# Two attention layers on eight images: output projections in another order, the norm among products, and the first attention begun on half of q and k

## The chip, the cores and the metric

The kernel runs on one core of one Trainium2 chip. Its time is the time on the device in microseconds (us), the median of several runs; the kernel before took 4062.5 us in the median of three runs (4062.24 to 4063.74). The profile is one execution, with a span of 4059.8 us from first to last instruction. TensorE (PE) multiplies matrices, VectorE (DVE), ScalarE (ACT) and GpSimd (POOL) do the rest, and SyncE (SP) issues nearly all transfers. [...]

## The reference, cut to what matters

Eight images of 32 x 32 positions with 512 channels, all fp32, go through two layers. Each normalises in 32 groups of channels, runs an attention over the 1024 positions and adds the result to its input.

```python
# layer 0: 16 heads of 32
xt = gn(x).reshape(B, N, C)
q, k, v = split_heads(xt @ w_qkv)
attn = softmax((q * 32 ** -0.5) @ k.T)
x = x + (attn @ v) @ w_proj + b_proj
# layer 1: 4 heads of 128, relative positions along both axes
q, k, v = gn(x) @ Wq / sqrt(128), gn(x) @ Wk, gn(x) @ Wv
scores = q @ k.T + relative_logits(q, pos_emb_w, pos_emb_h)
x = x + (softmax(scores) @ v) @ Wo
```

Each image has eight 512 x 512 projections: q, k, v and output in both layers.

## The kernel before

**Projections.** All activations lie with channels on the partitions, four chunks of 128 channels by 1024 positions. A projection is done in two half units, each by `seven` (L328): seven block products where a plain scheme has eight, on sums and differences of quarters ("forms", four VectorE operations in `forms`, L311 to L324, into three fixed buffers and in place). Unit u gives chunks u and u + 2 of the result. A product is eight matmuls, which the trace shows as 16 records (each fp32 matmul is recorded twice), in line L299. Around the products stand ScalarE copies of a half-done sum out of PSUM (p1, p7), VectorE adds (a, b) and the four adds or copies that give the result's quarters, by a "sink": `Plain` writes a new block, `Onto` (from L410) adds onto the residual. Half-done sums of products share three PSUM banks with other work. The pieces of weight for each product come from `Stream`, which loads them a unit ahead through 16 buffers, in the order of one list, `plan`; the list must match the order in which the units are done.

**First attention** (`attention_0`, L506): 64 steps, four chunks of heads by two halves of queries by eight blocks of keys. A step is scores `ps` (L516, eight matmul records, one PSUM buffer), an exponential `e` on ScalarE (L524, two buffers), the weighted sum of values `acc` (L535) and, on VectorE, the running sum of exponentials `es` (L544, L546). After eight steps `sums` (L556) and `normalise` (L482 to L504) divide the chunk. The second attention, `attention_1`, works likewise on heads of 128.

**Order of the work.** The main loop has nine iterations. Iteration b runs `attention_0(b)` side by side with a chain of other work. `side_by_side` (L782) advances the chain as far as a running account of costs allows: a product counts 2, the sum of the chain's costs is `total`, and after attention step n the chain may have used n/65 of it. What is left of the chain when the attention ends is done after it. In the middle iterations, the chain of before is:

1. the second layer's output projection of image b-2 (`after_1`; weights WO), at whose sixth product of the second unit a hook (`forms_0`) makes the forms of image b-1's first attention output
2. the first layer's output projection of image b-1 (`after_0`; WP), with the statistics for the norm
3. the norm of image b-1 (`norm_1`: store the block, ten small VectorE operations, and four L282 over the chunks), each of its pieces priced at ALONE = 5, so that only attention steps lie beside it
4. q, k, v of the second layer with the position logits (`second`; WQ1, WK1, WV1), starting with forms of the normed block
5. the second attention, woven with the loading, turning and norm of image b+1 (`load`)
6. q, k and v of the first layer for image b+1 (`before_0`), with a hook for the forms of the second attention's output

In front of the loop stands `before_0(0)`, so q, k and v of image 0 are done alone; iteration 0 then has the first attention of image 0 beside the loading of image 1 and its q, k, v. The residual inputs are stored in DRAM and come back by `fetch`, four transfers of 512 KB each, into blocks of which there are eight.

A scheduler puts the final order on each engine; it keeps to program order but for waits it can foresee and for stretches under `high_priority`.

Of the kernel before, what the change touches and what calls it, by code (L numbers as in the profile page):

```python
# [17 lines left out]
P = 128  # L18
# [9 lines left out]
def quick_path(  # L28
# [131 lines left out]
    class Stream:  # L160


        def __init__(self, plan):
            self.plan = [(m, rows, u) for m, rows in plan for u in range(2)]
            self.tiles = {}
            self.at = -1
            for i in ORDER:
                self.load(0, i)
# [77 lines left out]
    def group_norm(st, xT, name):  # L246

        mv = st.pop("mv")

        def averages(out, src, tag):  # L250
            total = small.tile([P, 2], F32, tag=f"total{tag}", name=f"total{tag}_{name}")
            nc.vector.tensor_reduce(
                total, src.rearrange("p (g k) -> p g k", k=GROUP_CHANNELS), axis=AX.X, op=ALU.add
            )
            nc.vector.tensor_scalar(
                out.rearrange("p (g k) -> p g k", k=GROUP_CHANNELS),
                total.unsqueeze(2).to_broadcast([P, 2, GROUP_CHANNELS]),
                1.0 / GROUP_CHANNELS,
                None,
                op0=ALU.mult,  # L260
            )

        turned = small.tile([P, 32], F32, tag="turned", name=f"turned_{name}")
        nc.vector.transpose(turned, mv)
        avg = small.tile([P, 2, 32], F32, tag="avg", name=f"avg_{name}")
        averages(avg[:, 0, :], turned, 0)

        nc.vector.tensor_sub(turned, turned, avg[:, 0, :])
        nc.vector.tensor_mul(turned, turned, turned)
        averages(avg[:, 1, :], turned, 1)  # L270
        back = small.tile([P, 2, 32], F32, tag="back", name=f"back_{name}")
        nc.vector.transpose(back.rearrange("p a c -> p (a c)"), avg.rearrange("p a c -> p (a c)"))
        mean = back[:, 0, :CC]
        var = small.tile([P, CC], F32, tag="var", name=f"var_{name}")
        nc.vector.scalar_tensor_tensor(
            var, back[:, 0, CC : 2 * CC], GN_EPS, back[:, 1, :CC], op0=ALU.add, op1=ALU.add
        )
        rstd = small.tile([P, CC], F32, tag="rstd", name=f"rstd_{name}")
        nc.gpsimd.tensor_tensor(rstd, var, neg_half, op=ALU.pow)
        yield 0  # L280
        for cc in range(CC):
            nc.vector.tensor_scalar(  # L282
                xT[cc],
                xT[cc],
                mean[:, cc : cc + 1],
                rstd[:, cc : cc + 1],
                op0=ALU.subtract,
                op1=ALU.mult,
            )
        yield 0  # L290


    in_place = [False]
# [31 lines left out]
    def snapshot(tag, name):  # L325
        return mem.tile([P, NB], F32, tag=tag, name=name, bufs=3 if tag == "e1" else 2)

    def seven(fs, u, rows, sink, name, hook=None):  # L328

        def product(out, i, start):
            w, f = stream.take(i), fs[i]
            if not rows:
                for c in range(HC):
                    by_columns(out, w[c], f[:, c, :], start and c == 0, c == HC - 1, True)
            else:
                for t in range(2):
                    for c in range(HC):  # L340
                        by_columns(
                            out[:, t * HN : (t + 1) * HN],
                            f[:, c, (2 * u + t) * P : (2 * u + t + 1) * P],
                            w[c],
                            start and c == 0 and t == 0,
                            c == HC - 1,
                            True,
                        )
            stream.ahead(i)

        x = bank(f"x_{name}")
        product(x, 0, True)
        p1 = snapshot("e1", f"p1_{name}")
        nc.scalar.copy(p1, x)
        yield HC
        y = bank(f"y_{name}")
        product(y, 5, True)
        a = snapshot("es1", f"a_{name}")
        nc.vector.tensor_add(a, y, p1)
        sink.early(p1, a)  # L360
        yield HC
        product(x, 1, False)
        sink.c11(x)
        yield HC
        product(y, 4, False)
        b = snapshot("es1", f"b_{name}")
        nc.vector.tensor_add(b, y, p1)
        sink.middle(b)
        yield HC
        z = bank(f"z_{name}")  # L370
        product(z, 6, True)
        p7 = snapshot("e1", f"p7_{name}")
        nc.scalar.copy(p7, z)  # L373
        yield HC
        product(y, 2, False)
        sink.c12(y, p1)
        if hook is not None:
            hook()
        yield HC
        product(z, 3, False)  # L380
        sink.c21(z, a)
        sink.c22(b, p7)
        yield HC

    class Plain:
# [64 lines left out]

        return [[x[n * HC + u][:, h * NB : (h + 1) * NB] for h in range(NH)] for n in range(2)]

    def project_T(fs, m, y, name):

        for u in range(2):
            stream.unit(m, False, u)
            yield from seven(fs, u, False, Plain(halves(y, u)), f"{name}_{u}")

# [46 lines left out]

    def attention_0(q, k, v, b):  # L506

        steps = [(m, h, j) for m in range(CC) for h in range(NH) for j in range(NT)]
        state = {}

        def front(m, h, j):
# [163 lines left out]
    def load(b, st):  # L675
# [19 lines left out]
        st["xn"] = forms(x, f"xn0_{b}")  # L695
        yield 0

    def before_0(b, st, hook=None):

        fs = st.pop("xn")  # L700
        st["q0"] = block(f"q0_{b}")
        st["q"] = chunks(st["q0"])
        yield from project_T(fs, WQ0, st["q"], f"q0_{b}")
        st["k"] = chunks(block(f"k0_{b}"))
        yield from project_T(fs, WK0, st["k"], f"k0_{b}")
        st["v"] = block(f"v0_{b}", [P, NT, C])
        yield from project_rows(fs, WV0, st["v"], f"v0_{b}", hook)
# [103 lines left out]
    PRODUCT = 2 * len(ORDER) * HC  # L811
    SECOND = 3 * PRODUCT - 8

    ALONE = 5

    WQ0, WK0, WV0 = [Matrix(w_qkv, i * C, f"qkv{i}") for i in range(3)]
    WP, WQ1, WK1 = Matrix(w_proj, 0, "p"), Matrix(Wq, 0, "q1"), Matrix(Wk, 0, "k1")
    WV1, WO = Matrix(Wv, 0, "v1"), Matrix(Wo, 0, "o")
    FIRST = [(WQ0, False), (WK0, False), (WV0, True)]
    plan = list(FIRST)  # L820
    for b in range(B + 1):
        if b == B:
            plan.append((WP, False))
        if b >= 2:
            plan.append((WO, False))
        if 1 <= b < B:
            plan.append((WP, False))
        if b >= 1:
            plan += [(WQ1, False), (WK1, False), (WV1, True)]
        if b + 1 < B:  # L830
            plan += FIRST
    plan.append((WO, False))

    states = [{} for _ in range(B)]
    WQ0.add_up(nc.vector, nc.scalar, nc.gpsimd, keep=True)
    run(load(0, states[0]))
    for m in (WK0, WV0):
        m.add_up(nc.vector, nc.sync, nc.gpsimd, keep=True)
    stream = Stream(plan)

# [2 lines left out]
            m.add_up(nc.gpsimd, nc.gpsimd, nc.gpsimd)  # L843
            yield 0

    run(before_0(0, states[0]))
    for b in range(B + 1):
        rest, total = [], 0
        s = [None] * 2 + states + [None] * 2
        past, last, here, coming = s[b : b + 4]  # L850
        incoming = load(b + 1, coming) if coming is not None else iter(())

        def forms_0(b=b, st=last):
            st["ao0"] = forms(st["q0"], f"ao0_{b - 1}")

        def forms_past(b=b, st=past):
            forms_1(b - 2, st)

        def forms_last(b=b, st=last):
            forms_1(b - 1, st)  # L860

        if last is not None:
            norm = norm_1(b - 1, last)
            if here is None:
                rest.append(after_0(b - 1, last, forms_past))
                rest.append(woven(later(after_1, b - 2, past), norm, 1, 4))
            else:
                if past is not None:
                    rest.append(after_1(b - 2, past, forms_0))
                    total += PRODUCT  # L870
                rest.append(later(after_0, b - 1, last))
                rest.append(chain([ALONE], (cost + ALONE for cost in norm), marked()))
                total += PRODUCT + 3 * ALONE
            rest.append(later(second, b - 1, last))
            rest.append(woven(later(lambda st: attention_1(*st.pop("at")), last), incoming, 4, 6))
            total += SECOND
        else:
            rest.append(incoming)
        if coming is not None:
            before = later(before_0, b + 1, coming, forms_last if last is not None else None)  # L880
            rest.append(before if last is not None else woven(before, other_sums(), 2, 7))
            total += 3 * PRODUCT
        if here is not None:
            side_by_side(attention_0(here["q"], here["k"], here["v"], b), chain(*rest), total)
        else:
            run(chain(*rest))
# [493 lines left out]
```

## Time and profile before

| engine | busy us | share | instructions |
|---|---|---|---|
| TensorE | 3848.8 | 95% | 30338 |
| VectorE | 2531.9 | 62% | 2915 |
| ScalarE | 1719.5 | 42% | 1761 |
| GpSimd | 601.6 | 15% | 396 |

| what | number of instructions | busy us |
|---|---|---|
| first attention: exponentials L524 | 512 | 961.6 |
| first attention: running sums L546 and L544 | 384 + 64 | 899.3 + 173.1 |
| TensorE's waits for exponentials ahead of scores L516 | 60 waits | 127.3 |
| DMA moved | 234.18 MB | mean 58 GB/s |

The busy time of an engine is the union of its instructions' times; matmuls overlap in it, so that a busy TensorE need not be one at its peak. In brackets behind an instruction stand the idle time of its engine just before it and what ended it. The granted clock (PEclk) is the share of full speed that TensorE's throttle allowed, 0.983 in the mean of the span.

### The profile page before, as it was taken

How to read it: one execution, taken by the hardware profiler on the slowest of the kernel's cores; microseconds unless marked ns; L12 is line 12 of the kernel's file. 1: busy time of each engine (PE TensorE's matmuls, PEld its weight loads, DVE VectorE, ACT ScalarE, POOL GpSimd, SP SyncE). 2: the span in 40 equal slices, each digit the busy share in tenths (PEclk: the TensorE clock that was granted, in tenths of full speed). 3: DMA queues.
4: the chain of work that ended last, by engine and by line, in shares of the span. 5: the costliest groups of instructions: out<-in, count | busy, mean ns of one | idle time of the engine just before them, and what ended most of it. 6: DMA issues, size and time to landing. Idle time of an engine off the chain costs nothing.

```text
span 4059.8 us, 71621 instructions
## 1 busy us (share of the span) xinstructions
PE 3848.8 (95%) x30338; PEld 1417.6 (35%) x30338; DVE 2531.9 (62%) x2915; ACT 1719.5 (42%) x1761; POOL 601.6 (15%) x396
## 2 busy tenths in 40 slices
PE   6898899998999989999999999999999998999998
PEld 3232244232443324432244323433234332244353
DVE  5776665576655867458564685646856568664544
ACT  1454443444434444344443444444444444543132
POOL 1331111121111211112110111101111111111101
PEclk9999999999999999999999999999999999999999
DMA  5320120141201512014120231203311031110401
GB/s 143 118 86 26 48 59 6 37 122 50 59 6 38 129 49 58 7 47 131 37 53 12 88 85 36 53 19 95 79 37 45 26 98 54 33 63 8 115 29 22
DMA packets 498694, 234.18 MB, mean 58 GB/s; under 512 B 286368, under 2 KB 478144, under 8 KB 497344
## 3 DMA queue, kind: packets, MB, share of 16 engines
q1 hardware_dynamic: 495232, 214.79, 19.8%
q0 software_dynamic: 2608, 13.70, 0.9%
q8 instruction: 241, 3.95, 0.4%
q10 hardware_dynamic: 528, 1.05, 0.1%
q14 instruction: 85, 0.70, 0.1%
HBM read 170.72 MB, written 58.72 MB: 57 GB/s over the span
## 4 chain that ended last, share of the span: by engine, by line
PE 86%; DVE 7%; ACT 5%; issue 1%; DMA 1%; POOL 0%; SPq 0%; DVEq 0%; ACTq 0%; POOLq 0%
PE ps L516 12%; PE ps L626 11%; PE acc L638 11%; PE acc L535 11%; PE y_q L299 4%; PE y_k L299 3%; PE y_v L299 3%; PE ps L627 3%; ACT e L524 3%; PE x_v L299 3%; PE x_k L299 3%; PE x_q L299 3%; PE z_q L299 3%; PE z_v L299 2%; PE z_k L299 2%; PE y_wp L299 2%
## 5 line engine op out<-in xcount | busy, mean ns | idle before, releaser
L524 ACT ACTIVATE e<-ps 128x2048 f32<-128x2048 f32 x512 | 961.6, 1878 | 873.4 <-PE ps L516 749.1
L546 DVE TENSOR_TENSOR es<-es,e 128x2048 f32<-128x2048 f32 x384 | 899.3, 2342 | 504.5 <-ACT e L524 503.0
L516 PE MATMUL ps<-q,k 32*128 32x512 f32 x4096 | 613.1, 654 | 127.5 <-ACT e L524 127.3
L535 PE MATMUL acc<-e,v 128*32 128x512 f32 x4096 | 557.5, 617 | 12.9 <-ACT su L482 11.9
L629 ACT ACTIVATE e<-ps 128x512 f32<-128x512 f32 x512 | 305.7, 597 | 581.4 <-PE ps L627 551.2
L626 PE MATMUL ps<-q,k 128*128 128x512 f32 x1024 | 523.7, 593 | 0.0
L638 PE MATMUL acc<-e,v 128*128 128x512 f32 x1024 | 521.9, 592 | 0.0
L649 DVE TENSOR_TENSOR es<-es,e 128x512 f32<-128x512 f32 x384 | 287.0, 747 | 267.3 <-ACT e L629 266.5
L627 PE MATMUL ps<-posT,sel 128*128 128x512 f32 x512 | 406.7, 794 | 0.0
L504 POOL TENSOR_TENSOR q<-q,su 128x512 f32<-128x512 f32 x128 | 199.2, 1557 | 1381.7 <-DVE su L500 1339.3
L516 PEld LDWEIGHTS ps<-q,k 32*128 32x128 f32 x4096 | 166.6, 186 | 533.4 <-ACT e L524 267.2
L626 PEld LDWEIGHTS ps<-q,k 128*128 128x128 f32 x1024 | 193.6, 190 | 246.2 <-issue 239.4
L638 PEld LDWEIGHTS acc<-e,v 128*128 128x128 f32 x1024 | 193.1, 189 | 146.7 <-issue 105.2
L535 PEld LDWEIGHTS acc<-e,v 128*32 128x32 f32 x4096 | 82.0, 109 | 409.3 <-issue 352.1
L612 DVE TENSOR_TENSOR posT<-pp,posT 32x512 fp32r<-32x512 f32 x128 | 111.2, 869 | 157.8 <-ACT posT L611 157.3
L544 DVE TENSOR_TENSOR es<-e,e 128x2048 f32<-128x2048 f32 x64 | 173.1, 2704 | 35.7 <-ACT e L524 35.7
L484 DVE STREAM_TRANSPOSE tu<-su 128x512 f32<-128x512 f32 x128 | 90.7, 709 | 116.3 <-ACT su L482 116.0
L611 ACT CAST posT<-pp 32x512 fp32r<-32x512 f32 x128 | 104.8, 819 | 132.2 <-DVE posT L612 87.4
L482 ACT COPY su<-sums 128x512 f32<-128x512 f32 x128 | 74.9, 585 | 160.2 <-PE sums L556 92.1
L408 POOL TENSOR_TENSOR v<-b_v,p_v 128x512 f32<-128x512 f32 x32 | 67.3, 2104 | 499.8 <-ACT p_v L373 479.3
L408 POOL TENSOR_TENSOR k<-b_k,p_k 128x512 f32<-128x512 f32 x32 | 64.0, 1999 | 513.7 <-ACT p_k L373 513.7
L627 PEld LDWEIGHTS ps<-posT,sel 128*128 128x128 f32 x512 | 97.3, 190 | 122.5 <-issue 122.5
(188 smaller groups left out, 4404.1 us busy)
## 6 DMA issues: line engine op xcount, KB each, us to landing
w_qkv<-ws_qkv SPq DMA_DIRECT2D x168, 128.0 KB, 2.5
xs<-in_x SPq DMA_DIRECT2D x256, 64.0 KB, 2.6
d<-x0T SPq DMA_DIRECT2D x32, 512.0 KB, 3.0
x1T<-d SPq DMA_DIRECT2D x32, 512.0 KB, 6.4
d<-x1T SPq DMA_DIRECT2D x32, 512.0 KB, 3.6
x2T<-d SPq DMA_DIRECT2D x32, 512.0 KB, 6.0
out<-ot SPq DMA_DIRECT2D x256, 64.0 KB, 2.0
w_qkv<-in_L_conv_w_qkv SPq DMA_DIRECT2D x126, 128.0 KB, 2.2
```

Source lines behind the costliest of these rows:

```text
L299: ins = nc.tensor.matmul(out[columns, :], weights[:, columns], moving, start=start, stop=stop, skip_group_check=open_sum,)
L504: nc.gpsimd.tensor_tensor(dst, dst, su, op=ALU.mult)
L516: nc.tensor.matmul(ps[:, r, :], k[m][rows, j * P : (j + 1) * P], q[m][rows, h * NB : (h + 1) * NB], start=True, stop=True,)
L524: nc.scalar.activation(e, ps, AF.Exp, scale=D0 ** -0.5)
L535: nc.tensor.matmul(acc[r * D0 : (r + 1) * D0, :], v[:, j, c0 : c0 + D0], e[:, r, :], start=(j == 0), stop=(j == NT - 1),)
L544: nc.vector.tensor_add(state["esum"], state["first"], e)
L546: nc.vector.tensor_add(state["esum"], state["esum"], e)
L626: nc.tensor.matmul(ps, k[h][:, keys], q[:, h, queries], start=True, stop=False)
L627: nc.tensor.matmul(ps, sel[:, keys], posT[:, h, queries], start=False, stop=True)
L629: nc.scalar.activation(e, ps, AF.Exp, scale=1.0 / math.sqrt(D1))
L638: nc.tensor.matmul(acc, v[:, j, h * D1 : (h + 1) * D1], e, start=(j == 0), stop=(j == NT - 1),)
L649: nc.vector.tensor_add(state["esum"], state["esum"], e)
```

## The change

The output projections change places: the first layer's, of image b-1, comes ahead of the second layer's, of image b-2. The norm of image b-1 then no longer has to stand between a projection and q of the second layer: it is woven into the second layer's output projection, from the fourth product on, a piece every third. The norm of a block comes in more pieces (a yield after every second chunk). Hooks move with that: the forms for `after_1` are made at the end of `after_0`, and those for `after_0` at the end of `before_0`, where the total of an iteration is cut by seven products so that the first attention ends ahead of them. Iteration 1 has no second-layer projection yet and keeps the norm alone (ALONE 4, four pieces).

In front of the loop, v and half of q and k of image 0 are done first; the attention takes its chunks in the order 0, 2, 1, 3, needing only the first unit's chunks for its first half, and the second half of q and k is done beside it, woven with the loading of image 1.

In `seven`, the copies and adds that read half-done sums are put down at a raised priority (SOON = 100).

```diff
-        yield 0
+            if cc % 2:
+                yield 0
...
+    SOON = 100
...
-        nc.scalar.copy(p1, x)
+        with tc.high_priority(SOON):
+            nc.scalar.copy(p1, x)
...
-        sink.c11(x)
+        with tc.high_priority(SOON):
+            sink.c11(x)
...
-        steps = [(m, h, j) for m in range(CC) for h in range(NH) for j in range(NT)]
+        steps = [(m, h, j) for m in (0, 2, 1, 3) for h in range(NH) for j in range(NT)]
...
+    def before_first(st):
+        fs = st["xn"]
+        st["v"] = block("v0_0", [P, NT, C])
+        yield from project_rows(fs, WV0, st["v"], "v0_0")
...
+        yield from project_T(fs, WQ0, st["q"], "q0_0", (0,))
+        yield from project_T(fs, WK0, st["k"], "k0_0", (0,))
+
+    def rest_of_first(st):
+        fs = st.pop("xn")
+        yield from project_T(fs, WQ0, st["q"], "q0_0", (1,))
+        yield from project_T(fs, WK0, st["k"], "k0_0", (1,))
...
-    ALONE = 5
+    ALONE = 4
...
-    run(before_0(0, states[0]))
+    run(before_first(states[0]))
...
         if last is not None:
             norm = norm_1(b - 1, last)
-            if here is None:
-                rest.append(after_0(b - 1, last, forms_past))
-                rest.append(woven(later(after_1, b - 2, past), norm, 1, 4))
+            rest.append(after_0(b - 1, last, forms_past if past is not None else None))
+            total += PRODUCT
+            if past is not None:
+                rest.append(woven(later(after_1, b - 2, past), norm, 3, 3))
+                total += PRODUCT
             else:
-                if past is not None:
-                    rest.append(after_1(b - 2, past, forms_0))
-                    total += PRODUCT
-                rest.append(later(after_0, b - 1, last))
                 rest.append(chain([ALONE], (cost + ALONE for cost in norm), marked()))
-                total += PRODUCT + 3 * ALONE
+                total += 4 * ALONE
             rest.append(later(second, b - 1, last))
+            total += SECOND
+            if here is not None and coming is None:
+                rest.append(at_once(forms_0))
+                total -= 4
             rest.append(woven(later(lambda st: attention_1(*st.pop("at")), last), incoming, 4, 6))
-            total += SECOND
         else:
-            rest.append(incoming)
+            rest.append(woven(rest_of_first(here), incoming, 0, 2))
+            total += PRODUCT
         if coming is not None:
-            before = later(before_0, b + 1, coming, forms_last if last is not None else None)
+            before = later(before_0, b + 1, coming, forms_0 if last is not None else None)
...
-            total += 3 * PRODUCT
+            total += 3 * PRODUCT - (PRODUCT // 2 if last is not None else 0)
```

More of the change, by code (lines that the diff above doesn't have):

```diff
@@ L163, in __init__ @@
         def __init__(self, plan):
-            self.plan = [(m, rows, u) for m, rows in plan for u in range(2)]
+            self.plan = plan
             self.tiles = {}
@@ L358, in seven @@
         a = snapshot("es1", f"a_{name}")
-        nc.vector.tensor_add(a, y, p1)
+        with tc.high_priority(SOON):
+            nc.vector.tensor_add(a, y, p1)
         sink.early(p1, a)
@@ L362, in seven @@
         product(x, 1, False)
-        sink.c11(x)
+        with tc.high_priority(SOON):
+            sink.c11(x)
         yield HC
@@ L366, in seven @@
         b = snapshot("es1", f"b_{name}")
-        nc.vector.tensor_add(b, y, p1)
+        with tc.high_priority(SOON):
+            nc.vector.tensor_add(b, y, p1)
         sink.middle(b)
@@ L372, in seven @@
         p7 = snapshot("e1", f"p7_{name}")
-        nc.scalar.copy(p7, z)
+        with tc.high_priority(SOON):
+            nc.scalar.copy(p7, z)
         yield HC
         product(y, 2, False)
-        sink.c12(y, p1)
+        with tc.high_priority(SOON):
+            sink.c12(y, p1)
         if hook is not None:
@@ L380, in seven @@
         product(z, 3, False)
-        sink.c21(z, a)
-        sink.c22(b, p7)
+        with tc.high_priority(SOON):
+            sink.c21(z, a)
+            sink.c22(b, p7)
         yield HC
@@ L451, in halves, with project_T @@
         return [[x[n * HC + u][:, h * NB : (h + 1) * NB] for h in range(NH)] for n in range(2)]
-    def project_T(fs, m, y, name):
-        for u in range(2):
+    def project_T(fs, m, y, name, units=(0, 1)):
+        for u in units:
             stream.unit(m, False, u)
@@ L696, in load @@
         yield 0
+    def before_first(st):
+        fs = st["xn"]
+        st["v"] = block("v0_0", [P, NT, C])
+        yield from project_rows(fs, WV0, st["v"], "v0_0")
+        st["q0"] = block("q0_0")
+        st["q"] = chunks(st["q0"])
+        st["k"] = chunks(block("k0_0"))
+        yield from project_T(fs, WQ0, st["q"], "q0_0", (0,))
[4 more added lines that the diff above has]
+        yield from project_T(fs, WK0, st["k"], "k0_0", (1,))
     def before_0(b, st, hook=None):
@@ L818, in quick_path, with units @@
     WV1, WO = Matrix(Wv, 0, "v1"), Matrix(Wo, 0, "o")
-    FIRST = [(WQ0, False), (WK0, False), (WV0, True)]
-    plan = list(FIRST)
+    def units(m, rows=False):
+        return [(m, rows, u) for u in range(2)]
+    FIRST = units(WQ0) + units(WK0) + units(WV0, True)
+    plan = units(WV0, True) + [(m, False, u) for u in range(2) for m in (WQ0, WK0)]
     for b in range(B + 1):
-        if b == B:
-            plan.append((WP, False))
+        if b >= 1:
+            plan += units(WP)
         if b >= 2:
-            plan.append((WO, False))
-        if 1 <= b < B:
-            plan.append((WP, False))
+            plan += units(WO)
         if b >= 1:
-            plan += [(WQ1, False), (WK1, False), (WV1, True)]
+            plan += units(WQ1) + units(WK1) + units(WV1, True)
         if b + 1 < B:
             plan += FIRST
-    plan.append((WO, False))
+    plan += units(WO)
     states = [{} for _ in range(B)]
-    WQ0.add_up(nc.vector, nc.scalar, nc.gpsimd, keep=True)
+    WV0.add_up(nc.vector, nc.scalar, nc.gpsimd, keep=True)
     run(load(0, states[0]))
-    for m in (WK0, WV0):
+    for m in (WQ0, WK0):
         m.add_up(nc.vector, nc.sync, nc.gpsimd, keep=True)
@@ L844, in other_sums, with at_once @@
             yield 0
-    run(before_0(0, states[0]))
+    def at_once(do):
+        do()
+        return
+        yield
+    run(before_first(states[0]))
     for b in range(B + 1):
@@ L851, in quick_path, with forms_0 @@
         incoming = load(b + 1, coming) if coming is not None else iter(())
-        def forms_0(b=b, st=last):
-            st["ao0"] = forms(st["q0"], f"ao0_{b - 1}")
+        def forms_0(b=b, st=here):
+            st["ao0"] = forms(st["q0"], f"ao0_{b}")
         def forms_past(b=b, st=past):
             forms_1(b - 2, st)
-        def forms_last(b=b, st=last):
-            forms_1(b - 1, st)
         if last is not None:
             norm = norm_1(b - 1, last)
-            if here is None:
-                rest.append(after_0(b - 1, last, forms_past))
-                rest.append(woven(later(after_1, b - 2, past), norm, 1, 4))
-            else:
-                if past is not None:
-                    rest.append(after_1(b - 2, past, forms_0))
-                    total += PRODUCT
-                rest.append(later(after_0, b - 1, last))
+            rest.append(after_0(b - 1, last, forms_past if past is not None else None))
[3 more added lines that the diff above has]
+                total += PRODUCT
+            else:
                 rest.append(chain([ALONE], (cost + ALONE for cost in norm), marked()))
-                total += PRODUCT + 3 * ALONE
+                total += 4 * ALONE
             rest.append(later(second, b - 1, last))
+            total += SECOND
+            if here is not None and coming is None:
+                rest.append(at_once(forms_0))
+                total -= 4
             rest.append(woven(later(lambda st: attention_1(*st.pop("at")), last), incoming, 4, 6))
-            total += SECOND
         else:
-            rest.append(incoming)
+            rest.append(woven(rest_of_first(here), incoming, 0, 2))
+            total += PRODUCT
         if coming is not None:
-            before = later(before_0, b + 1, coming, forms_last if last is not None else None)
+            before = later(before_0, b + 1, coming, forms_0 if last is not None else None)
             rest.append(before if last is not None else woven(before, other_sums(), 2, 7))
-            total += 3 * PRODUCT
+            total += 3 * PRODUCT - (PRODUCT // 2 if last is not None else 0)
         if here is not None:
```

## The prediction, made before the result was known

> **What bounds the kernel now.** I read the page first: busy time by engine, the 40 slices, the chain that ended last.
>
> ```profile
> PE 3848.8 (95%) x30338; PEld 1417.6 (35%) x30338; DVE 2531.9 (62%) x2915; ACT 1719.5 (42%) x1761; POOL 601.6 (15%) x396
> ...
> PE   6898899998999989999999999999999998999998
> ...
> PE 86%; DVE 7%; ACT 5%; issue 1%; DMA 1%; POOL 0%; SPq 0%; DVEq 0%; ACTq 0%; POOLq 0%
> ```
>
> TensorE carries 86% of the chain. An edit that adds no product and removes none can only win what TensorE does not use: its idle and slow-clock time. I therefore took prices from distances between starts where TensorE is dense (busy times of matmuls overlap): a product takes 1.83 us ahead of scores (926.35 to 928.18 below) and 1.72 ahead of another product, which I use; scores take 1.07, weighted sum of values 1.00 (a little less ahead of a product), and 0.86 for the sums of an attention part. One step of the first attention costs 2.07 of TensorE.[...]
>
> Where attention runs alone, a step takes 3.14 us, not 2.07 (359.93 to 363.07): scores have one PSUM buffer, so the next scores wait for the exponential.
>
> ```profile
> 359.93 1.14 PE L516 MATMUL ps<-q,k 32*128 32x512 f32 x8 [1.00 <-ACT e L524]
> 361.00 1.06 PE L535 MATMUL acc<-e,v 128*32 128x512 f32 x8
> 363.07 1.14 PE L516 MATMUL ps<-q,k 32*128 32x512 f32 x8 [1.00 <-ACT e L524]
> ```
>
> Then the second norm, TensorE's timeline in iteration 2 (start, length, what; in brackets idle before and what ended it):
>
> ```profile
> 926.35 1.90 PE L299 MATMUL z_wp<-q,w_p 128*32 128x512 f32 x16
> 928.18 1.14 PE L516 MATMUL ps<-q,k 32*128 32x512 f32 x8
> ...
> 938.14 1.14 PE L516 MATMUL ps<-q,k 32*128 32x512 f32 x8 [1.00 <-ACT e L524]
> 939.21 1.06 PE L535 MATMUL acc<-e,v 128*32 128x512 f32 x8
> 946.76 2.09 PE L516 MATMUL ps<-q,k 32*128 32x512 f32 x8 [6.48 <-ACT e L524]
> 948.77 1.94 PE L535 MATMUL acc<-e,v 128*32 128x512 f32 x8
> 950.48 3.13 PE L299 MATMUL x_q<-x1T,w_q 128*32 128x512 f32 x16
> ```
>
> and the same place by windows (window, length, busy of TensorE, weight loads, VectorE, ScalarE, GpSimd with counts, granted clock, DMA share, GB/s), beside a dense one:
>
> ```profile
> 860.00:920.00 60.00, 60.00 (x528) 16.23 (x521) 51.35 (x51) 25.52 (x20) 13.19 (x9) 1.00 0.51 102
> 928.18:950.48 22.30, 13.81 (x76) 2.97 (x76) 19.38 (x28) 8.21 (x6) 3.23 (x3) 0.75 0.20 77
> ```
>
> Between the last product of the output projection and the first of the next q, 22.30 us hold four scores, four weighted sums and one sums: 4 x 2.07 + 0.86 = 9.1. So 13.2 us are lost, and the cold first product loses 3.13 - 1.90 = 1.2 more: **14.4 us for each norm**. VectorE works 19.38 of these 22.30: the adds onto the residual, statistics, norm and forms, with the attention's running-sum add queued behind them.
>
> [...] after 6.48 us of idle, scores took 2.09 instead of 1.14; gaps of 1.00 do not do that. [...] the running-sum add at 942.45 starts as the second form add ends, and the exponential that needs its buffer starts at 944.83. [...] two adds at 142.54 took 8.51 us together instead of 2 x 2.29, beside GpSimd's sums of weights. That bears on iteration 0.
>
> **The change, part by part.**
>
> *Norm among products.* Before, in iterations 1 to 7, the norm has only attention steps beside it (the three yields are priced at ALONE = 5, 15 in all). After, for b = 2 to 7, the first layer's projection comes first and the norm is woven into the 14 products of the second layer's output projection, three yields apart; q of the second layer then starts several products later than the norm's end. The same products and steps remain, so up to 14.4 comes back, six times. What can remain is VectorE. Its ledger for the two projections: the iteration's cost falls from 231 to 202 over 65 steps, 3.1 a step, 1.55 products at cost 2, so 28 products spread over 18 steps. TensorE: 28 x 1.72 + 18 x 2.07 + 2.25 x 0.86 = 87.4. VectorE: running-sum adds 15.75 x 2.29 = 36.1; normalising 2.25 x 1.9 = 4.3; adds of four half units 4 x (2 x 0.68 + 4 x 0.74) = 17.3; statistics 5.9; norm 2.2 of small operations + 4 x 0.73 = 5.1; transposes for the output 8 x 0.70 = 5.6; two sets of forms at 1.2 an operation, 9.5. Sum 83.8, **96% of TensorE's time**. It fits, but without room, and it comes in bursts: forms of the second projection, last adds, statistics and norm stand together, some 12 to 13 us between two running-sum adds. Two buffers of exponentials and one of scores cover about 9 us of that at this density (two steps of 2.07 + 1.55 x 1.72 = 4.7), so some 3 us of waiting[...]: **4.4 us left**. Bounds: 0 (if the scheduler puts the adds between) and 8.2 (the full stall of before: 939.21 to 946.76 is 7.55, less 1.00 of work, plus 1.65 by which the scores and sums after it were slower than 2.07). Six times (14.4 - 4.4) = **-60**. b = 1 has no second projection, keeps ALONE (16 instead of 15): 0, bounds +-3.
>
> *First attention begun on half of q and k.* Iteration 0 runs from its first scores (108.38) to the point where products are dense again (379.46, first product of the output projection): 271.1 us. Its work: 64 x 2.07 + 8 x 0.86 + 42 products x 1.72 + about 5.5 for the first product and scores after it = 217; **54 us idle**, most of it attention alone at the end as at 359.93 and beside the load's VectorE work at the start. After, v and half of q and k come first (28 products), attention begins 14 x 1.72 = 24.1 earlier, and 14 products more lie beside its 64 steps: 56 for 64, nearly one each. A step with a product needs 3.79 > 3.14, so idle by the one score buffer vanishes. What stays: first step 2, load and norm bursts on VectorE 5 to 8, GpSimd's weight sums against VectorE's adds about 10 (six to eight adds stretched as at 142.54), last parts, forms and the cold clock 7: about 30. Total work is the same; the gain is 54 - 30 = **-24**. Bounds: -12 if half the steps end up alone, -34 if GpSimd's part shrinks with the denser steps.
>
> *Forms of the attention output ahead of the iteration's end.* The iteration's total is cut by seven products so attention ends seven before; the forms (4.7 us) and the last normalising (about 5.5) lie under 7 x 1.72 = 12.0 us of v's products. Before, the forms lay under a later projection; so 0, bounds 0 to +2 each.
>
> *Fetches.* Both residual blocks now come together at the boundary, eight transfers of 512 KB which wait for blocks freed by the attention before. The page has about 6 us from issue to landing for each kind. They are needed by the first adds onto the residual, which have two buffers of snapshots and three banks in hand; weights are loaded a unit of seven products (12 us and more with steps) ahead. I take 0; bounds 0 to 10 each.
>
> *Readers of half-done sums first* (SOON). Orders copies and adds that free PSUM ahead of others. It can shorten waits such as 2.88 us for scores at 1010.90, beside the position logits, where a second product now stands ahead of the scores: about -0.9 an image, **-6** in all; bounds -15 and +8 (exponentials pushed behind copies).
>
> *The end* (b = 8): order there is as before, small waits only: 0, +-5.
>
> Sum: 4062.5 - 60 - 24 - 6 = **3972.5**.
>
> **Rivals.** *B: VectorE becomes the bound* in the stage with both projections. For: 96% of ledger, [...]two buffers. Against: in 860 to 920 it does 51.35 of 60 and TensorE does not lose a thing. Then 10 us a period stay and half of iteration 0's gain: 4062.5 - 6 x 4.4 - 12 = 4024. *C: nothing is left of the norm*, since adds between its yields pass, and iteration 0 loses only 20: 4062.5 - 6 x 14.4 - 34 - 8 = 3934. For: the three yields are spread. Against: the burst above. *D: slower.* The boundary takes over the stall: TensorE waits for the forms as at 375.87 to 379.46, with cold start about 7.5 us, and 4 MB of fetches at the 300 to 369 GB/s that the DMA slices show at the boundary of before (840 to 855) hold weights back by some 10: 7 x 17.5 = 122, less 90: 4095. Against: 12 us of products over the forms, and the DMA share of 0.51 in the dense window without a wait.
>
> **How the numbers follow.** Forecast 0.66, B 0.16, C 0.13, D 0.05. The time is the forecast's, 3973. The range 3932 to 4026 takes in B and C at their centres (each with half of its spread beyond) and leaves D: about 2 in 10 outside. Faster 0.94 (all but D and a margin), same 0.01, slower 0.05.
>
> **What would show it.** Right: TensorE's idle before the first x_q of each image near 0, no granted clock of 0.75 there; the scores' wait for exponentials, which sums now to 127.3 us, down by more than half; the output projection of image 0 starting some 24 us earlier; steps of iteration 0 near 3.8. Wrong: waits of scores of 6 us and more now among the wo products (B), or waits of the first y_wp for forms or of adds for x1T and x2T at each boundary (D). The forecast fails if the running-sum adds queue behind copies raised by SOON, which no view of before shows.

## The result, and the profile after

The changed kernel takes 4017.8 us in the median (4016.85 to 4019.54); the kernel before took 4062.4 beside it. The ratio is 0.989, with a 95% interval of 0.987 to 0.991: 44.6 us faster, half of the 89.5 that the forecast had. The time lies in the range given, and on its slow side, at the rival B (4024).

The top of the page, as for the kernel before (busy by engine, TensorE's slices, the chain that ended last):

```profile
PE 3836.2 (95%) x30338; PEld 1405.4 (35%) x30338; DVE 2528.6 (63%) x2915; ACT 1721.6 (43%) x1761; POOL 605.6 (15%) x396
...
PE   6999999999999999999999999999999998999898
...
PE 84%; DVE 9%; ACT 4%; issue 1%; POOL 1%; SPq 0%; DMA 0%; DVEq 0%; POOLq 0%; ACTq 0%
```

Work did not change, so the totals say little. The chain tells the direction: VectorE's share of it rose from 7% to 9%. The waits of TensorE (what waited, for what, total, times, longest) tell more:

```profile
PE ps L529 <- ACT e L537: 42.8, 34, 7.6
PE y_wo L301 <- DVE a_wo L367: 40.0, 7, 8.0
PE x_v L301 <- DVE x0T L283: 31.7, 1, 31.7
PE sums L569 <- ACT q L562: 16.1, 5, 3.2
PE acc L548 <- ACT su L495: 10.3, 6, 1.7
PE y_q L301 <- DMA w_q<-ws_q: 8.0, 1, 8.0
```

The scores' wait for exponentials fell from 127.3 to 42.8 us, as forecast. (The 31.7 is the first product's wait at the start, which was there before.) But three waits have grown: that of a product of the second output projection for the add `a`, 40.0 us in seven waits (1.6 before), that of the sums for a copy of `q` on ScalarE, 16.1 (1.5 before), and that of products of q for their weights at the end, 8.0 (3.3 before).

Where the 42.0 us of span between the two traces (4059.8 and 4017.8) lie, from the starts of the first products of each stage:

| stretch | before | after | difference | forecast |
|---|---|---|---|---|
| start to first `y_wp` | 379.5 | 352.1 | -27.3 | -24 |
| iteration 1, to the next first output projection | 468.6 | 466.1 | -2.5 | 0 +-3 |
| iterations 2 to 6 | 2462.5 | 2441.0 | -21.5 (4.3 each) | -50 and -5 |
| iteration 7 | 431.8 | 435.6 | +3.8 | -10 and -1 |
| the end | 317.4 | 323.0 | +5.6 | 0 +-5 |

In the first row, one product of the output projection (1.7 us) that stood ahead of the first `y_wp` before stands behind it now; for the same work the gain is 25.6.

The middle images in detail. I call lost what a distance between two starts has over the price that the forecast took from dense stretches. Before, an image loses 14.4 us at the norm and about 9 beside the position logits (q, k, v of the second layer: 9.1 in the mean of five). After, it loses 9 in the second output projection, where the norm now is, and 10 beside the position logits. TensorE in iteration 3 of the changed kernel:

```profile
1353.78 1.14 PE L529 MATMUL ps<-q,k 32*128 32x512 f32 x8
1354.85 1.07 PE L548 MATMUL acc<-e,v 128*32 128x512 f32 x8
1355.73 1.90 PE L301 MATMUL x_wo<-q,w_o 128*32 128x512 f32 x16
1363.89 3.64 PE L301 MATMUL y_wo<-f_ao,w_o 128*32 128x512 f32 x16 [6.26 <-DVE a_wo L367]
1367.46 1.72 PE L529 MATMUL ps<-q,k 32*128 32x512 f32 x8
```

After the idle 6.26 the clock is slow too: the granted clock was 0.50 from 1363.89 to 1367.46, and the product at 1363.89 takes 3.57 to the next start instead of the 1.83 of a product ahead of scores. Why `a_wo` is late stands in VectorE's timeline at the same place:

```profile
1344.77 2.28 DVE L559 TENSOR_TENSOR es<-es,e 128x2048 f32<-128x2048 f32 x1
1346.97 0.74 DVE L438 SCALAR_TENSOR_TENSOR x1T<-p_wp,bproj_sb,x1T 128x512 f32<-128x512 f32 x1
...
1353.11 0.15 DVE L265 STREAM_TRANSPOSE turned<-mv 128x32 f32<-128x32 f32 x1
...
1357.84 3.19 DVE L283 TENSOR_SCALAR x1T<-x1T,back,rstd 128x1024 f32<-128x1024 f32 x3 [1.20 <-POOL rstd L280]
1360.96 2.28 DVE L557 TENSOR_TENSOR es<-e,e 128x2048 f32<-128x2048 f32 x1
1363.16 0.68 DVE L367 TENSOR_TENSOR a_wo<-y_wo,p_wo 128x512 f32<-128x512 f32 x1
```

The product that `a_wo` reads ended about 1353.8, and the add needs 0.68. It stands behind the whole chain of the norm (from 1353.11), three of the four normalising operations and a running-sum add, and comes 9.4 us late. The next product into the same PSUM bank waited for it, with 6.26 of idle. In the program, `a` is put down ahead of the norm's first operation, and at the raised priority; the scheduler set it behind all the same.

### The profile page after: what moved, and what is told of

Read it like the earlier page. It is cut to its first block, busy times and chain, and to the rows that moved or that the text cites. A ratio compares the mean times of both kernels' runs of the same rounds, so it can differ in the third digit from the quotient of the medians.

```text
span 4017.8 us, 71580 instructions
## 1 busy us (share of the span) xinstructions
PE 3836.2 (95%) x30338; PEld 1405.4 (35%) x30338; DVE 2528.6 (63%) x2915; ACT 1721.6 (43%) x1761; POOL 605.6 (15%) x396
## 4 chain that ended last, share of the span: by engine, by line
PE 84%; DVE 9%; ACT 4%; issue 1%; POOL 1%; SPq 0%; DMA 0%; DVEq 0%; POOLq 0%; ACTq 0%
PE ps L529 12%; PE ps L639 11%; PE acc L651 11%; PE acc L548 10%; PE y_q L301 4%; PE y_v L301 4%; PE ps L640 3%; PE y_k L301 3%; PE x_v L301 3%; PE x_k L301 3%; PE x_q L301 3%; PE z_q L301 2%; ACT e L537 2%; PE z_v L301 2%; PE y_wo L301 2%; PE z_k L301 2%
## 5 line engine op out<-in xcount | busy, mean ns | idle before, releaser
L559 DVE TENSOR_TENSOR es<-es,e 128x2048 f32<-128x2048 f32 x384 | 887.7, 2312 | 458.7 <-ACT e L537 457.9
L529 PE MATMUL ps<-q,k 32*128 32x512 f32 x4096 | 598.8, 650 | 42.9 <-ACT e L537 42.8
L624 ACT CAST posT<-pp 32x512 fp32r<-32x512 f32 x128 | 105.0, 820 | 127.3 <-DVE posT L625 83.5
L301 PE MATMUL y_wo<-f_ao,w_o 128*32 128x512 f32 x768 | 110.8, 649 | 45.8 <-DVE a_wo L367 40.0
L660 DVE TENSOR_TENSOR es<-e,e 128x512 f32<-128x512 f32 x64 | 44.2, 690 | 146.1 <-ACT e L642 146.1
```

Source lines behind the costliest of these rows:

```text
L301: ins = nc.tensor.matmul(out[columns, :], weights[:, columns], moving, start=start, stop=stop, skip_group_check=open_sum,)
L529: nc.tensor.matmul(ps[:, r, :], k[m][rows, j * P : (j + 1) * P], q[m][rows, h * NB : (h + 1) * NB], start=True, stop=True,)
L559: nc.vector.tensor_add(state["esum"], state["esum"], e)
```

## The experiments

All ratios are to the kernel before on the same chip, with 95% intervals.

**Only the early start.** The kernel before with this part alone: `before_first`, `rest_of_first`, the order of chunks, the plan of weights.

```diff
-    run(before_0(0, states[0]))
+    run(before_first(states[0]))
...
-            rest.append(incoming)
+            rest.append(woven(rest_of_first(here), incoming, 0, 2))
+            total += PRODUCT
```

> Before, with only the early start of the first attention (v and half of q and k ahead, the other half beside it). Theory: this part gives what the stage shows, first product of the output projection 27 us earlier, and nothing later: 4062.4 - 27 = 4035, and the second norm still loses 14.4 us an image. Rival: part of the 27 us is due to the new order of projections or to the raised priorities, and this part alone gives less than 20: above 4042.

Measured 4037.5 us, 0.9943 (0.9930 to 0.9957). The first `y_wp` starts at 353.9 instead of 379.5, and the q behind that output projection 24.5 us earlier; the 1.1 between the two is less than the one product that has moved behind the first `y_wp` here too. The norm's idle of the later images is as before. So this part is 23 of the 45 us, and it stands alone.

**Without the raised priority.**

```diff
-        with tc.high_priority(SOON):
-            sink.c11(x)
+        sink.c11(x)
```

and likewise at the other places.

> After, without the raised priority. Theory: the priority covers the sinks, and with them the output transfers at the end, which now all stand ahead of weights for q on SyncE's queue; without it the 8 us wait for those weights returns to about 4, so the end gets 4 to 6 us shorter, and the steady images stay within 1 us each: 4010 to 4018. Rival: the priority saves waits beside the position logits, 1 to 2 us an image, so that the kernel without it is slower: 4020 to 4028.

Measured 4013.7, 0.9882 (0.9867 to 0.9897): not to be told from the changed kernel (0.9874 to 0.9908) by time. The trace tells the place. The sink `Onto` also issues the output (`then`), so the priority covers the output's transfers. In the changed kernel, all 32 of the last image but one stand in a row on SyncE's queue, ahead of weights for q:

```profile
3728.31 30.04 SPq L789 DMA_DIRECT2D out<-ot  x32
3758.45 0.98 SPq L191 DMA_DIRECT2D w_q<-ws_q  x2
```

Not all of the 30.04 us is work: one issue takes 0.50 us in the median. Three times in this stretch SyncE waits for a transpose that the next transfer reads (for what, total, times, longest):

```profile
SPq L789 <- DVE ot L786: 13.2, 3, 5.9
```

The first weights behind are issued at 3758.45. Without the priority, some go between the transfers:

```profile
3727.36 17.45 SPq L781 DMA_DIRECT2D out<-ot  x20
3744.91 0.46 SPq L191 DMA_DIRECT2D w_q<-in_L_conv_Wq  x1
```

The wait for weights of q there falls from 8.00 to 4.00 us. Beside the position logits the loss is the same with and without the priority, 10 us an image: there it is worth nothing.

**The norm held in program order.** Same operations; the norm's first operation and the four L283 are kept behind what was put down ahead of them on VectorE (by then, the adds `a` and `b` of the first half unit).

```diff
-        nc.vector.transpose(turned, mv)
+        keep(nc.vector.transpose(turned, mv))
...
-            nc.vector.tensor_scalar(
+            keep(nc.vector.tensor_scalar(
...
+        keep = tc.keep_in_program_order if b >= 1 else lambda ins: ins
-        yield from group_norm(st, xT, f"1_{b}")
+        yield from group_norm(st, xT, f"1_{b}", keep)
```

> After, with the second norm's operations on VectorE (images 1 to 6 and 7) held behind what stands ahead of them in the program: the adds a and b of the first half unit and the running-sum adds issued by then. Theory (queue): the 9 us that each image still loses in the second output projection are the add a and the first running-sum add standing behind the norm's chain; they fall below 3 for each of six images, 4018 - 6 x 7 = 3976, and between 3970 and 3990. Rival (capacity): VectorE has no room in this stage whatever the order, the wait turns up some products later with the same size: 4013 to 4023.

Measured 3971.9, 0.9778 (0.9765 to 0.9792), within what the theory of the queue gave, near its lower end. VectorE has the same work (2528.4 us busy, 2528.6 in the changed kernel) and now this order:

```profile
1348.87 2.25 DVE L557 TENSOR_TENSOR es<-e,e 128x2048 f32<-128x2048 f32 x1
1351.04 0.68 DVE L367 TENSOR_TENSOR a_wo<-y_wo,p_wo 128x512 f32<-128x512 f32 x1
...
1356.17 0.67 DVE L377 TENSOR_TENSOR b_wo<-y_wo,p_wo 128x512 f32<-128x512 f32 x1
...
1357.40 0.16 DVE L265 STREAM_TRANSPOSE turned<-mv 128x32 f32<-128x32 f32 x1
```

and TensorE does not stop (starts in the same place of the work):

```profile
1350.63 1.90 PE L301 MATMUL x_wo<-q,w_o 128*32 128x512 f32 x16
1352.35 1.90 PE L301 MATMUL y_wo<-f_ao,w_o 128*32 128x512 f32 x16
1354.18 1.14 PE L529 MATMUL ps<-q,k 32*128 32x512 f32 x8
```

The waits for `a_wo` sum to 4.4 us instead of 40.0:

```profile
PE y_wo L301 <- DVE a_wo L367: 4.4, 9, 1.0
```

Iterations 2 to 6 take 2409.7 us, 6.3 an image less than in the changed kernel, and iteration 7 takes 423.5 instead of 435.6. What stays of the norm's 14.4 is 2 to 3 us an image. The rival that VectorE has no room is refuted, for it does the same work (2528.4 us busy) with 4.4 us of waits for `a_wo`, not 40.0. From the start of the first output projection to that of q in iteration 3 (window, length, busy of TensorE, weight loads, VectorE, ScalarE, GpSimd, granted clock, DMA):

```profile
1301.60:1389.30 87.70, 87.27 (x756) 23.28 (x756) 76.47 (x88) 40.65 (x30) 26.21 (x15) 1.00 0.33 84
```

VectorE is busy for 76.47 of 87.70 us, 87%; the 96% of the forecast's ledger was too high.

**The four normalising operations on ScalarE.**

```diff
-                nc.vector.tensor_scalar(
-                    xT[cc], xT[cc], mean[:, cc : cc + 1], rstd[:, cc : cc + 1],
-                    op0=ALU.subtract, op1=ALU.mult,
-                )
+                nc.scalar.activation(
+                    xT[cc], xT[cc], AF.Identity,
+                    bias=shift[:, cc : cc + 1], scale=rstd[:, cc : cc + 1],
+                )
```

The `shift` is one small operation more on VectorE.

> After, with the four normalising operations of the second norm (images 1 to 7) on ScalarE instead of VectorE, and one small operation more on VectorE; same result. Theory (queue): three of the four stood ahead of the add a, 3.2 us for the three, so each of six images gains 3 to 3.5 us: about 3998. Rival: the exponentials are held up by the four operations on ScalarE, about 1 us each, and nothing is gained: 4012 to 4025.

Measured 4002.3, 0.9856 (0.9841 to 0.9871): the 15 us that the shorter queue gives, but not for the reason alone that I had. The wait moves to the other engine's queue: TensorE's next product now waits 3.89 us for the copy `p_wo`, which starts at 1355.77 behind the first of these operations on ScalarE; that one starts at 1354.62, after 6.68 of idle that ended with `shift` on VectorE.

```profile
1356.39 3.64 PE L315 MATMUL x_wo<-q,w_o 128*32 128x512 f32 x16 [3.89 <-ACT p_wo L375]
```

**Held in order, and no raised priority.** The two edits above together.

> After, with the norm's VectorE operations held in program order and without the raised priority. Theory: the two add up, since one acts on VectorE in the middle images and the other on SyncE's queue at the end: 3972 less 4 to 5, 3967; the last wait for weights of q falls from 10 us of loss to about 6. Rival: the raised priority is what lets the adds pass once the norm is out of the way, and without it the pinned kernel loses 1 us or more an image: above 3976.

Measured 3973.2, 0.9784 (0.9770 to 0.9797): neither of the two numbers, the same as with the priority within the noise. In the trace q's stage at the end loses 6.0 us instead of 10.4, but the time doesn't show these 4 us: the runs of this kernel span 3968.8 to 3977.4.

**Held in order, the priority kept but for the output.** The sink's `then` is called after the block with raised priority.

```diff
-            self.then(n, h)
+            late.append((n, h, self.then))
```

> The pinned kernel with the raised priority kept on copies and adds, but taken off the output's transposes and transfers. Theory: what the priority costs at the end is the order of SyncE's queue alone, so this equals the pinned kernel without any raised priority, 3967 within 2. Rival: the copies and adds themselves matter, and the end stays at 10 us of loss in q's stage: 3972.

Measured 3967.1, 0.9766 (0.9752 to 0.9779), at the theory's number, but its interval overlaps with both kernels above, so the time does not decide. By the trace, q's last stage loses 2.5 us, less than in both, with a wait of 1.41 for weights. That what the priority costs at the end is the order of the output's transfers is shown by the traces, not by the times; that the priority is worth anything is not shown.

**Casts ahead of subtractions.** What is left to lose is the position logits, 10 us an image. For each group, four casts on ScalarE and four subtractions on VectorE stood by turns. In the changed kernel, ScalarE's timeline in iteration 3:

```profile
1524.10 1.08 ACT L624 CAST posT<-pp 32x512 fp32r<-32x512 f32 x1 [1.38 <-PE pp L612]
1526.28 0.58 ACT L624 CAST posT<-pp 32x512 fp32r<-32x512 f32 x1 [1.11 <-DVE posT L625]
1527.62 1.07 ACT L624 CAST posT<-pp 32x512 fp32r<-32x512 f32 x1 [0.76 <-DVE posT L625]
1529.78 0.58 ACT L624 CAST posT<-pp 32x512 fp32r<-32x512 f32 x1 [1.10 <-DVE posT L625]
1530.38 1.88 ACT L537 ACTIVATE e<-ps 128x2048 f32<-128x2048 f32 x1
```

Each cast but the first waits for the subtraction before it (1.11, 0.76 and 1.10 us), though they write different partitions or columns, and the exponential stands behind them all: 6.3 us for 3.3 us of casts. Why the program makes them wait was not taken apart. In TensorE's timeline the sums then wait for the copy of `q` behind that exponential:

```profile
1532.79 1.93 PE L569 MATMUL sums<-es,ones 128*32 128x512 f32 x8 [3.23 <-ACT q L562]
```

The edit, on the held kernel without priority:

```diff
-                    nc.scalar.copy(view[rows], pp[rows])
-                    nc.vector.tensor_sub(view[rests], pp[rows], view[rows].bitcast(F32))
+            for view, rows, rests in turns:
+                nc.scalar.copy(view[rows], pp[rows])
+            for view, rows, rests in turns:
+                nc.vector.tensor_sub(view[rests], pp[rows], view[rows].bitcast(F32))
```

> The pinned kernel without raised priority, with the position logits' four casts on ScalarE put ahead of their four subtractions on VectorE (same operations, same result). Theory: each cast waits for the subtraction before it by turns, a chain of some 6 us that holds the exponential behind it; of 10 us that each image loses in k and v of the second layer 4 or more go, seven images: 3967 - 30 = 3937, at most 3950. Rival: VectorE's or ScalarE's work in that stage is the limit, not the turns, and less than 1 us an image goes: above 3960.

Measured 3917.9, 0.9647 (0.9634 to 0.9661), more than the theory gave: iterations 2 to 6 take 2370.7 us instead of 2409.8, 7.8 an image, and iterations 1 and 7 gain as well (4.7 and 9.4); the end does not. The four casts now run without a wait:

```profile
1496.66 3.29 ACT L621 CAST posT<-pp 32x512 fp32r<-32x512 f32 x4 [1.43 <-PE pp L604]
1499.98 1.88 ACT L529 ACTIVATE e<-ps 128x2048 f32<-128x2048 f32 x1
```

**The same edit on the kernel before, and on the changed kernel.**

> Before, with the four casts of the position logits ahead of their four subtractions, nothing else. Theory: the turns between ScalarE and VectorE cost about 7 of the 9 us that each image of before loses in k and v of the second layer, whatever the order of the projections: 4062 - 7 x 6.5 = 4016, between 4010 and 4030. Rival: the turns only cost in the order of after, where the groups fall on steps with one product: above 4045.

Measured 4000.8, 0.9850 (0.9837 to 0.9864): 61 us, more than the whole change, and more than was expected. An image of before loses 2 us instead of 9 in k and v; iterations 2 to 6 are 2425.0 us instead of 2462.5.

> After, with the casts ahead of the subtractions. Theory: adds to the change without regard to the norm's queue, 50 us less as between the two pinned kernels: 3968, between 3960 and 3978. Rival: the wait for the norm's queue takes up part of it: above 3985.

Measured 3964.0, 0.9757 (0.9744 to 0.9770): the 54 us add to the change, and its second output projection still loses 9 us an image for the norm's queue. The two are nearly independent: together they gain 98 us, apart 45 and 61.

**All together**: held in order, casts first, priority but for the output.

> All that gained together: after, the norm held in program order, casts ahead of subtractions, raised priority for copies and adds but not for the output's transposes and transfers. Theory: the priority is worth nothing else than the few us at the end, so this is 3918 less 3 to 5: 3913 to 3916. Rival: with the casts grouped, the raised priority of adds sets them ahead of running sums in the position stage and loses there: above 3922.

Measured 3914.5, 0.9636 (0.9623 to 0.9649), at the theory's number and the fastest here, though its interval overlaps with that of the kernel with casts first and no priority. TensorE's granted clock is 0.996, from 0.983 before.

## Why the prediction was half right

*Early start*: right. Scores begin at 85.2 instead of 108.4 (forecast 24.1 earlier, measured 23.2), and from there to the first `y_wp` it takes 266.9 us for work that the forecast's prices put at 217 + 13 x 1.72 = 239 (13 products more than before stand ahead of that point): some 28 us idle, forecast 30. How much of the idle time belongs to GpSimd's sums of weights is not shown: beside such sums in the kernel before, the add at 137.84 took 2.35 us and the two at 142.54 took 8.51, and the 10 us that the forecast put down for them were its author's estimate.

*Norm among products*: this is the step that failed. The mechanism held (products cover the norm, and what remains is a VectorE burst), and the burst was sized well: forecast 12 to 13 us between two running-sum adds, measured 1347.05 to 1360.96, 13.9. But the term "4.4 us left" was 9. Of the 4.4, 1.4 for a slower clock after the wait were the author's estimate (the product at 1363.89 alone took 3.57 instead of 1.83). The other 3 came from a slack of 9 us in the buffers of exponentials and scores, of which two things were left out. First, the add after the burst (2.28) and the exponential that needs its buffer (1.88) follow before scores can start: the exponential begins at 1363.33 and ends at 1365.2, where TensorE, unstopped, would have reached those scores about 1359.3 (an estimate: 1355.73 + 1.72 + 1.83). That alone is some 6 us. Second, a different waiter comes earlier: the adds `a` and `b`, which free a PSUM bank, stand in VectorE's queue as well, and a product waited for `a`, which started at 1363.16, from 1357.6 on. I had followed only the running-sum add. In the program `a` and `b` are put down ahead of the norm; that the scheduler would set them behind it, no view of before shows, and only the lower bound of the forecast spoke of the scheduler's order. No run takes out one of the two waiters alone, so how the 9 us divide between them is not shown. Of the forecast -10 an image the changed kernel got about -5 at the norm; when the held order takes both waiters out, the middle images gain 10.6 each over before (2409.7 against 2462.5). That the forecast time of 3973 is met by that kernel doesn't make the forecast right: it had the gain without the edit that it needs.

In iteration 7 the same step failed more. There the wait for `a` is 8.0, and by the same prices both output projections lose 18 us against 20 before, where the forecast had 10 less. Fewer products stand there for each attention step, and I had used the density of the middle images; that this is the reason is not shown. The stretch from k to the second attention loses some 5 us more than before, so that the iteration is 3.8 longer; that was not taken apart.

*Readers of half-done sums first*: forecast -6, with bounds of -15 and +8. Beside the position logits the changed kernel loses 1 us an image more than before, not 0.9 less. The experiment without the priority has the same 10 us, so the cause is not the priority; before with the early start alone keeps its 9, so it comes with the new order of projections. How it does was not taken apart further, since the turns behind it (7 to 8 us in either order) are the larger thing.

*The end*: forecast 0 +-5, measured +5.6. I took the order there to be as before. The priority moved the output's transfers ahead of weights (without it, the end takes 316.1 us), which I had not followed from `add` through `then` to SyncE's queue.

*The clock*: the forecast says that gaps of 1.00 us do not slow TensorE. That was read wrongly. The same timeline of before has, between the lines at 929.25 and 938.14,

```profile
931.32 1.12 PE L516 MATMUL ps<-q,k 32*128 32x512 f32 x2 [1.00 <-ACT e L524]
932.37 1.87 PE L556 MATMUL sums<-es,ones 128*32 128x512 f32 x8
934.17 1.97 PE L516 MATMUL ps<-q,k 32*128 32x512 f32 x6
```

with a granted clock of 0.53 from 932.4 to 936.0, and at 1010.90, after 2.88 of idle, scores took 2.04, with a granted clock of 0.52. So the length of the last gap alone does not tell, and how long an idle time slows the clock is not shown. The 14.4 us come from distances between starts and stand.

*Forms and fetches at the iteration's boundary*: right. The stretch from the last products of v to the first of the output projection loses below 1 us in every middle image; rival D did not happen. Rival B gave nearly the measured time, but its mechanism, VectorE without room, is refuted by the held kernel; what held TensorE up was the order in VectorE's queue (3971.9 us in the held kernel against 4017.8).

## What to carry to other kernels

When small operations are moved beside dense TensorE work, list every reader of PSUM that may stand behind them in the same engine's queue, not only the largest (here `a_wo`, 9.4 us late), and add to the burst the time of what must still follow it (here an add of 2.28 us and an exponential of 1.88) before TensorE can go on. Where the place in the queue matters, hold the order in the program, since the scheduler may choose another. A ledger of load alone did not tell whether the work fits: the order was worth 46 us at the same work (4017.8 against 3971.9). And operations of two engines that write one tile by turns deserve a look: putting all of one engine's first gave 61 us on the kernel before, more than the 45 of the whole change.

## What the runs showed of the hardware that I had not expected

Four casts of 32 x 512 on ScalarE took 3.29 us in a row (casts first, on the held kernel) and 6.3 by turns with VectorE's subtractions (changed kernel, iteration 3), with 0.76 to 1.11 us of waiting at each turn. SyncE's queue stood still for output transfers whose source was not ready: 32 of them took 30.04 us in the changed kernel, 13.2 of these in waits for transposes on VectorE, and TensorE then waited 8.00 us for weights for q issued behind them. TensorE's clock was slow (0.53 from 932.4 to 936.0 in the kernel before) where the gap just ahead was only 1.00 us.
